# Expert tiles of a mixture-of-experts layer: from transposes on the matrix engine to transposing loads of 16-bit halves

## The chip, the cores and the metric

The kernel runs on one core of a Trainium2 chip. The metric is device microseconds (us) of one execution. A core has engines that run side by side, each through its own list of instructions in order: TensorE (PE in the profile, with its weight loads as PEld), VectorE (DVE), ScalarE (ACT), GpSimd (POOL) and SyncE (SP), which here only issues DMA transfers. Transfers are carried by 16 DMA engines that all issuers share.

## The reference, cut to what matters

The reference takes 16,384 tokens of 256 numbers (32 blocks of 512) through three parts.

```
h = tokenizer(x)                                  # a DFT of patches and a matrix, here one set of matmuls
h = h + retention_and_mlp(layernorm(h))           # q, k, v, a decaying scan, relu MLP 256 -> 1024 -> 256
tokens = layernorm(h)                             # float32, 256 features
combine = weights of the best 2 of 8 experts      # softmax of tokens @ router_w.T, top 2, renormalized
out = tokens
for e in range(8):
    y = gelu(tokens @ w1[e] + b1[e]) @ w2[e] + b2[e]
    out = out + combine[:, e:e+1] * y
h = h + out
```

Every token goes to two experts, so the expert part handles 32,768 rows.

## The kernel before, in words

**Blocks.** The tokens are worked on in 32 blocks of 512 (`TT` = 4 groups of 128 partitions). The main loop has 34 iterations; in each, three blocks are at different stages: a new one is embedded and goes through retention, a middle one through the MLP, an old one is routed. The order of instructions on SP, PE, DVE and ACT is the order of the Python code (a schedule written out by hand); POOL's is left to the planner.

**Where expert rows come from.** At the end of the MLP (`mlp_out`, L345 to L375) the normalized tokens are written to the tile `tok` (L363, L364), which has 260 numbers per token: 256 features and four more, the key of the first expert, two shares and the token's number. `choose` and `place` (L393 to L477) work out which two experts a token goes to and at which row of the scratch buffer `xbuf` in HBM it belongs. Eight indirect DMAs per block, issued by POOL (L450), scatter the 1,040-byte rows into `xbuf`, where each expert has a region of its own.

**Expert tiles.** `take` (L496) cuts the filled parts of the regions into tiles of 256 rows (135 in all) and appends them to a list. `expert_step` (L637) advances the list by one tile. In step n it runs:

- `load` (L556) of the tile three places ahead. SP reads the expert's and the row's offset from a table, issues the load of the rows as `xg` (L561; 260 KB, rows on the partitions, six buffers) and then the load of the expert's weights `w` (L566; 641.5 KB, five buffers).
- `turn` (L568) of tile n+1: four PE transposes of 128x128 (L572) bring the rows into features-first order in PSUM, and one ACT copy (L574) takes them to `xT`.
- `enter` (L576) of tile n: eight matmuls (L581), and the Gelu on ACT (L589).
- `leave` (L593) of tile n-1: eight matmuls (L598); DVE works out each row's share (L607, L610) from the extra numbers in `xg`, adds the bias and scales (L612, L614) into `y` (two buffers); POOL issues two indirect DMAs (L618) that add the rows of `y` to `out` in HBM, at the token numbers in `xg`. The two adds of a tile wait until both adds of the tile before have landed (L616), so that no sum is lost.

An `xg` buffer is free again when the adds of its tile have landed, because these read the token numbers from it. A `w` buffer is free when L612 has read the output bias from it.

**Steps in an iteration.** While there is a new block, `slot` (L651) runs an expert step in each of four places, as long as more than 12 tiles are waiting: after `embed`, after the fourth `mlp_in`, after the retention and after `residual`. Once no blocks are left, the remaining tiles are worked off one after another (L710). A backlog of about 12 tiles and the last block's 18 are therefore done near the end.

**Around `mlp_out`.** At the end of an iteration the order of ACT's list is: the two `ks` activations of the retention, the expert steps' copies and Gelus; then, at the start of the next iteration, the copy `ms` (L262), which frees a PSUM buffer of the pool `p_tm` (three buffers) and lets DVE form the new block's `h` (L276); the two `hT` activations of `features2` (L221), then the two `tokT` copies of `features3` (L215), which free buffers of the pool `p_mm` (four). `turn`, `enter`, `features2`, `features3` and every `feature_mm` take their PSUM tiles from `p_mm` in turn.

Of the kernel before, what the change touches and what calls it, by code (L numbers as in the profile page):

```python
# [11 lines left out]

F32 = mybir.dt.float32
I32 = mybir.dt.int32
AF = mybir.ActivationFunctionType
ALU = mybir.AluOpType
AX = mybir.AxisListType

P = 128
# [10 lines left out]
def vit_tower_kernel(  # L30
# [15 lines left out]
    nc = tc.nc  # L46
    B, NBLK, _, XW = x.shape
    D = wtok.shape[1]
# [3 lines left out]
    KD, KH = D // P, H // P  # L52
    J = STRIDE // 2
    TT = 4
# [8 lines left out]
    S = 2 * P  # L63
# [3 lines left out]
    RW = D + 4  # L67
# [166 lines left out]
    class Block:  # L234
# [110 lines left out]
        def mlp_out(self, u):  # L345
            if u == 0:
                self.norm = Norm()
            ps = p_tm.tile([P, 2, D], F32, name="tm")
            for i in range(2):
                for k in range(KH):  # L350
                    nc.tensor.matmul(  # L351
                        ps[:, i, :],
                        lhsT=self.aT[:, k, ts(u * 2 + i, P)],
                        rhs=w2_sb[:, k, :],
                        start=k == 0,
                        stop=k == KH - 1,
                    )
            nc.vector.tensor_tensor(self.h[:, ts(u, 2), :], ps, self.h[:, ts(u, 2), :], ALU.add)  # L358
            for i in range(2):
                self.norm.stats(self.h, u * 2 + i)  # L360
            if u == U - 1:
                self.norm.factors()
                self.tok = two.tile([P, TT, RW], F32, name="tok")  # L363
                self.norm.apply(self.tok, self.h)  # L364
                nc.vector.tensor_tensor(self.h, self.h, self.tok[:, :, :D], ALU.add)

                to = out[ts(self.i, BLK), :].rearrange("(u q r) d -> q u (r d)", q=P, r=2)
                self.stored = nc.sync.dma_start(out=to, in_=self.h.rearrange("p (u r) d -> p u (r d)", r=2))
                unordered("sums", self.stored, ())
                nc.gpsimd.iota(  # L370
                    self.tok[:, :, NUMBER : NUMBER + 1].bitcast(I32),
                    pattern=[[2 * P, U], [1, 2]],
                    base=self.i * BLK,
                    channel_multiplier=2,
                )  # L375
# [17 lines left out]
        def choose(self):  # L393

            ps = self.lg
            shape = [P, TT, E]

            def wide(a):
                return a.unsqueeze(2).to_broadcast(shape)

            lg = small.tile(shape, F32, name="lg")
            top = small.tile([P, TT], F32, name="top")
            first_key = self.tok[:, :, FIRST]
            nc.vector.tensor_copy(lg, ps)
            nc.vector.tensor_reduce(top, lg, AX.X, ALU.max)
            nc.vector.tensor_tensor(lg, lg, wide(top), ALU.subtract)
            key = small.tile(shape, F32, name="key")
            self.oh = oh = small.tile([P, 2, TT, E], F32, name="oh")
            nc.vector.scalar_tensor_tensor(key, lg, 0.0, key0, ALU.is_equal, ALU.mult)
            nc.vector.tensor_reduce(first_key, key, AX.X, ALU.max)  # L410
            nc.vector.tensor_tensor(oh[:, 0], key, wide(first_key), ALU.is_equal)
            nc.vector.scalar_tensor_tensor(lg, oh[:, 0], -3.0e38, lg, ALU.mult, ALU.add)
            second = small.tile([P, TT], F32, name="second")
            nc.vector.tensor_reduce(second, lg, AX.X, ALU.max)
            nc.vector.tensor_tensor(key, lg, wide(second), ALU.is_equal)
            nc.vector.tensor_tensor(key, key, key0, ALU.mult)
            nc.vector.tensor_reduce(top, key, AX.X, ALU.max)
            nc.vector.tensor_tensor(oh[:, 1], key, wide(top), ALU.is_equal)
            self.both = small.tile(shape, F32, name="both")
            nc.vector.tensor_tensor(self.both, oh[:, 0], oh[:, 1], ALU.add)  # L420
            self.ex = small.tile([P, TT], F32, name="ex")
            nc.gpsimd.tensor_tensor(self.ex, euler, second, ALU.pow)

        def place(self):
# [5 lines left out]
            before = small.tile([P, TT, E], F32, name="before")  # L430
            nc.vector.tensor_copy(before[:, 0, :], cnt)
            for t in range(TT):
                to = cnt if t == TT - 1 else before[:, t + 1, :]
                nc.vector.tensor_tensor(to, ps[:, 1, t, :], before[:, t, :], ALU.add)
            nc.vector.tensor_tensor(before, ps[:, 0], before, ALU.add)
            nc.vector.tensor_tensor(oh, oh, before.unsqueeze(1).to_broadcast([P, 2, TT, E]), ALU.mult)
            row = small.tile([P, 2, TT], I32, name="row")
            rowf = small.tile([P, 2, TT], F32, name="rowf")
            nc.vector.tensor_reduce(rowf, oh, AX.X, ALU.add)
            nc.vector.tensor_copy(row, rowf)  # L440

            share = small.tile([P, TT], F32, name="share")
            nc.vector.tensor_scalar(share, self.ex, 1.0, None, ALU.add)
            nc.vector.reciprocal(share, share)
            nc.vector.tensor_tensor(self.tok[:, :, SECOND], share, self.ex, ALU.mult)
            nc.vector.tensor_tensor(self.tok[:, :, DIFF], share, self.tok[:, :, SECOND], ALU.subtract)
            writes = []
            for t in range(TT):
                for c in range(2):
                    write = nc.gpsimd.indirect_dma_start(  # L450
                        out=xbuf,
                        out_offset=bass.IndirectOffsetOnAxis(ap=row[:, c, t : t + 1], axis=0),
                        in_=self.tok[:, t, :],
                        in_offset=None,
                    )
                    unordered("rows", write, ())
                    writes.append(write)
            if self.i == 0:
                spare = xbuf[E * REG :, :].rearrange("(i p c) d -> p i (c d)", i=SPARE, p=P)
                to = none.rearrange("p c d -> p (c d)").unsqueeze(1).to_broadcast([P, SPARE, 2 * RW])  # L460
                write = nc.sync.dma_start(out=spare, in_=to)
                unordered("rows", write, ())
                writes.append(write)
                write = nc.sync.dma_start(
                    out=out[NTOK:, :].rearrange("(p c) d -> p c d", p=P), in_=none[:, :, :D]
                )
                unordered("sums", write, ())
            if self.i == NB - 1:
                ends = small.tile([1, E], I32, name="ends")
                nc.vector.tensor_copy(ends, cnt[0:1, :])  # L470
                for e in range(E):
                    end = nc.sync.value_load(ends[:, e : e + 1], min_val=e * REG, max_val=e * REG + NTOK)
                    to = xbuf[bass.ds(end, S), :].rearrange("(p c) d -> p c d", p=P)
                    write = nc.sync.dma_start(out=to, in_=none)
                    unordered("rows", write, ())
                    writes.append(write)
            return writes  # L477
# [13 lines left out]
        after(what, others)  # L491
        tc.add_to_no_dep_group(name, what.ins)

    xbuf = dram.tile([ROWS, RW], F32, name="xbuf")

    def take(n, block, writes):  # L496

# [52 lines left out]
    class Tile:  # L550
# [5 lines left out]
        def load(self):  # L556
            t = self.t
            wrow = nc.sync.value_load(self.table[:, 0, t : t + 1], min_val=0, max_val=(E - 1) * P)
            row = nc.sync.value_load(self.table[:, 1, t : t + 1], min_val=0, max_val=ROWS - S)
            self.xg = six.tile([P, 2, RW], F32, name="xg")  # L560
            read = nc.sync.dma_start(  # L561
                out=self.xg, in_=xbuf[bass.ds(row, S), :].rearrange("(c p) d -> p c d", p=P)
            )
            unordered("rows", read, self.writes)
            self.w = five.tile([P, NW], F32, name="w")
            nc.sync.dma_start(out=self.w, in_=wex[bass.ds(wrow, P), :])  # L566

        def turn(self):  # L568
            ps = p_mm.tile([P, KD, 2, P], F32, name="mm")
            for k in range(KD):  # L570
                for c in range(2):
                    nc.tensor.transpose(ps[:, k, c, :], self.xg[:, c, ts(k, P)], ident)  # L572
            self.xT = two.tile([P, KD, S], F32, name="xT")
            nc.scalar.copy(self.xT, ps.rearrange("p k c q -> p k (c q)"))  # L574

        def enter(self):  # L576
            self.ge = two.tile([P, KD, S], F32, name="ge")
# [15 lines left out]
        def leave(self):  # L593
            w = self.w
            ps = p_tm.tile([P, 2, D], F32, name="tm")
            for c in range(2):
# [8 lines left out]
            share = small.tile([P, 2], F32, name="tile_share")  # L605
            tag = w[:, 5 * D + KD : 5 * D + KD + 1]
            nc.vector.scalar_tensor_tensor(  # L607
                share, self.xg[:, :, FIRST], tag, self.xg[:, :, DIFF], ALU.is_equal, ALU.mult
            )
            nc.vector.tensor_tensor(share, share, self.xg[:, :, SECOND], ALU.add)  # L610
            y = two.tile([P, 2, D], F32, name="y")
            nc.vector.tensor_tensor(y, ps, w[:, 4 * D : 5 * D].unsqueeze(1).to_broadcast([P, 2, D]), ALU.add)  # L612
            for c in range(2):
# [3 lines left out]
            for c in range(2):  # L617
                add = nc.gpsimd.indirect_dma_start(  # L618
                    out=out,
                    out_offset=bass.IndirectOffsetOnAxis(  # L620
                        ap=self.xg[:, c, NUMBER : NUMBER + 1].bitcast(I32), axis=0
                    ),
                    in_=y[:, c, :],
                    in_offset=None,
# [169 lines left out]
```

## Time and profile before

| what | value |
|---|---|
| median of three executions | 2452.55 us (2449.38 to 2454.42) |
| profiled execution, its own time | 2448.38 us |
| span of the profiled execution (first to last instruction) | 2446.4 us |
| PE busy | 2298.4 us (94%) |
| DVE busy | 1347.3 us (55%) |
| POOL busy | 930.1 us (38%) |
| ACT busy | 556.7 us (23%) |
| moved by DMA | 256.44 MB, mean 105 GB/s |

Busy time is a share of the whole span, and the stages of this kernel have different limits, so the table alone does not tell what sets the end. The page's strip of 40 slices shows each engine's busy share over the span in tenths. The answers on a stretch of the timeline list instructions with start, duration, engine and line; "idle before" behind an instruction says how long its engine had waited and for whom. A busy time of PE includes the modelled end of the last matmul, which lies over the start of the next group, so what a group takes from PE's time is better read from the distance between starts.

### The profile page before, as it was taken

The numbers are of one execution on the slowest core, as the hardware profiler recorded it, in microseconds if no ns is written. First come the engines' busy times: TensorE is split into PE (matmuls) and PEld (weight loads), VectorE is DVE, ScalarE is ACT, GpSimd is POOL, SyncE is SP. The second block draws the span as 40 slices with busy tenths as digits, with TensorE's granted clock in tenths as the row PEclk, the third lists the DMA queues.
The fourth block names the chain that finished last, engine by engine and source line by source line (L and its number), as shares of the span: only waits on it lengthen the run. The fifth ranks groups of instructions, "written<-read, shape, count | busy, mean of one in ns | idle before, by whom it ended". The sixth has DMA issues, their size and how long they took to land. (4 is left out here: it accounts for less than half of the span.)

```text
span 2446.4 us, 29049 instructions
## 1 busy us (share of the span) xinstructions
PE 2298.4 (94%) x9740; PEld 1687.8 (69%) x9740; DVE 1347.3 (55%) x4111; ACT 556.7 (23%) x952; POOL 930.1 (38%) x845
## 2 busy tenths in 40 slices
PE   3999999999999999999999999999999999986673
PEld 2677666777777777777777777777777777665553
DVE  6566665565655555655555556555555665533221
ACT  0122222222222222222222222222222222221221
POOL 0022222344444334444443344444433444335444
PEclk8999999999999999999999999999999999998887
DMA  4021121333344343333443433334334333347674
GB/s 140 18 79 59 56 105 64 98 89 102 109 122 116 103 110 101 89 102 109 122 113 105 112 101 89 102 109 122 111 107 111 102 90 85 91 106 208 168 182 86
DMA packets 128181, 256.44 MB, mean 105 GB/s; under 512 B 14497, under 2 KB 88097, under 8 KB 123937
## 3 DMA queue, kind: packets, MB, share of 16 engines
q1 hardware_dynamic: 76864, 185.09, 23.3%
q0 software_dynamic: 51168, 69.50, 15.3%
q8 instruction: 77, 1.26, 0.2%
q14 instruction: 72, 0.58, 0.1%
HBM read 164.04 MB, written 90.50 MB: 104 GB/s over the span
## 5 line engine op out<-in xcount | busy, mean ns | idle before, releaser
L618 POOL DMA_INDIRECT out<-y,xg x270 | 426.1, 1578 | 587.6 <-DVE y L614 386.9
L229 PE MATMUL mm<-hT,w_sb 128*128 128x512 f32 x1024 | 478.3, 600 | 0.0
L351 PE MATMUL tm<-w_sb,aT 128*128 128x256 f32 x2048 | 453.0, 379 | 0.0
L351 PEld LDWEIGHTS tm<-w_sb,aT 128*128 128x128 f32 x2048 | 388.5, 190 | 54.9 <-issue 2.4
L450 POOL DMA_INDIRECT xbuf<-tok,row x256 | 314.4, 1228 | 238.1 <-DVE whole L506 161.5
L229 PE MATMUL mm<-hT,wqkv_sb 128*128 128x512 f32 x768 | 338.1, 596 | 0.1
L612 DVE TENSOR_TENSOR y<-tm,w 128x512 f32<-128x512 f32 x135 | 93.3, 691 | 382.8 <-PE tm L598 226.9
L229 PEld LDWEIGHTS mm<-hT,w_sb 128*128 128x128 f32 x1024 | 184.6, 190 | 158.4 <-issue 155.4
L581 PE MATMUL mm<-xT,w 128*128 128x256 f32 x1080 | 275.9, 401 | 3.5 <-DVE ret L313 2.3
L191 POOL TENSOR_SCALAR rstd<-mv 128x4 f32<-128x4 f32 x96 | 37.1, 387 | 635.8 <-DVE mv L185 635.8
L343 ACT ACTIVATE aT<-mm,vec 128x512 f32<-128x512 f32 x256 | 175.9, 687 | 395.2 <-PE mm L229 392.6
L229 PEld LDWEIGHTS mm<-hT,wqkv_sb 128*128 128x128 f32 x768 | 143.9, 191 | 169.6 <-issue 154.1
L598 PE MATMUL tm<-w,ge 128*128 128x256 f32 x1080 | 258.4, 383 | 0.0
L269 PE MATMUL tm<-weff,xd 128*128 128x256 f32 x1024 | 233.4, 382 | 8.5 <-DVE xd L246 8.5
L581 PEld LDWEIGHTS mm<-xT,w 128*128 128x128 f32 x1080 | 206.2, 201 | 34.6 <-DVE ret L313 9.2
L598 PEld LDWEIGHTS tm<-w,ge 128*128 128x128 f32 x1080 | 209.1, 194 | 29.9
L269 PEld LDWEIGHTS tm<-weff,xd 128*128 128x128 f32 x1024 | 191.1, 192 | 32.7 <-DVE xd L246 8.9
L574 ACT COPY xT<-mm 128x512 f32<-128x512 f32 x135 | 79.0, 585 | 531.3 <-PE mm L572 528.2
L589 ACT ACTIVATE ge<-mm,w 128x256 f32<-128x256 f32 x270 | 113.1, 470 | 182.7 <-PE mm L581 157.2
L572 PE MATMUL mm<-ident,xg 128*128 128x128 f32 x540 | 85.1, 282 | 64.9 <-DMA xg<-xbuf 64.8
L258 PE MATMUL tm<-wsum,xb 128*128 128x256 f32 x512 | 118.3, 385 | 25.8 <-ACT wsum L115 25.8
L358 DVE TENSOR_TENSOR h<-tm,h 128x512 f32<-128x512 f32 x64 | 44.0, 687 | 174.8 <-PE tm L351 174.8
(112 smaller groups left out, 2277.2 us busy)
## 6 DMA issues: line engine op xcount, KB each, us to landing
w<-in_wex SPq DMA_DIRECT2D x135, 641.5 KB
xg<-xbuf SPq DMA_DIRECT2D x135, 260.0 KB
xb<-in_x SPq DMA_DIRECT2D x32, 1040.0 KB
out<-h SPq DMA_DIRECT2D x32, 512.0 KB
out<-y,xg POOLq DMA_INDIRECT x270
xbuf<-tok,row POOLq DMA_INDIRECT x256
xbuf<-none SPq DMA_DIRECT2D x8, 260.0 KB
w_sb<-in_w SPq DMA_DIRECT2D x2, 1024.0 KB
```

The source lines that it names most:

```text
L229: nc.tensor.matmul(ps, lhsT=w[:, k, ts(m, P)], rhs=rhs[:, k, :], start=k == 0, stop=k == KD - 1)
L258: nc.tensor.matmul(ps[:, u, :], lhsT=od[:, j, ts(u, P)], rhs=wsum[:, j, :], start=j == 0, stop=j == J - 1)
L269: nc.tensor.matmul(ps[:, i, :], lhsT=xd[:, i, j, ts(u, P)], rhs=weff[:, i * J + j, :], start=j == 0, stop=j == J - 1,)
L343: nc.scalar.activation(self.aT[:, m, :], ps, AF.Relu, bias=vec[:, MB1 + m : MB1 + m + 1])
L351: nc.tensor.matmul(ps[:, i, :], lhsT=self.aT[:, k, ts(u * 2 + i, P)], rhs=w2_sb[:, k, :], start=k == 0, stop=k == KH - 1,)
L450: write = nc.gpsimd.indirect_dma_start(out=xbuf, out_offset=bass.IndirectOffsetOnAxis(ap=row[:, c, t : t + 1], axis=0), in_=self.tok[:, t, :],
L572: nc.tensor.transpose(ps[:, k, c, :], self.xg[:, c, ts(k, P)], ident)
L581: nc.tensor.matmul(ps[:, m, :], lhsT=self.w[:, k * D + m * P : k * D + (m + 1) * P], rhs=self.xT[:, k, :], start=k == 0, stop=k == KD - 1,)
L589: nc.scalar.activation(self.ge[:, m, :], ps[:, m, :], AF.Gelu, bias=self.w[:, 5 * D + m : 5 * D + m + 1])
L598: nc.tensor.matmul(ps[:, c, :], lhsT=self.ge[:, k, ts(c, P)], rhs=w[:, (2 + k) * D : (3 + k) * D], start=k == 0, stop=k == KD - 1,)
L612: nc.vector.tensor_tensor(y, ps, w[:, 4 * D : 5 * D].unsqueeze(1).to_broadcast([P, 2, D]), ALU.add)
L618: add = nc.gpsimd.indirect_dma_start(out=out, out_offset=bass.IndirectOffsetOnAxis(ap=self.xg[:, c, NUMBER : NUMBER + 1].bitcast(I32), axi ...
```

## The change

The rows of `xbuf` are stored in another form, and are read back already turned.

- In `mlp_out` the normalized tokens go to `tok` without the four extra numbers and with one buffer instead of two. ACT then makes a second tile, `row`, of the same 1,040 bytes per token: the first 512 bytes hold the upper 16-bit halves of the 256 features, the next 512 bytes the lower halves, the last 16 bytes the four extra numbers. This takes two ACT copies of 16-bit words per block, of 128x1024 each (new L371), with a stride of two words on the reading side. The row writes take `row` instead of `tok`.
- `load` issues three transfers instead of two: a transposing load of the two planes of 16-bit words (256 rows of 512 words) into `xh`, laid out 128 partitions x 4 x 256 (six buffers); then `w`; then a load of only the four extra numbers of each row into `xg` (16 bytes a row).
- `turn` has no PE instruction any more. Two ACT copies of 128x512 16-bit words put the upper and the lower halves of the features together in `xT` (new L580), with a stride of two words on the writing side.
- The shares and the token numbers are read from the small `xg`. Names change in `place` (`row` to `to`, `to` to `upto`); the arithmetic does not.

```diff
@@ mlp_out
-                self.tok = two.tile([P, TT, RW], F32, name="tok")
+                self.tok = one.tile([P, TT, D], F32, name="tok")
                 self.norm.apply(self.tok, self.h)
-                nc.vector.tensor_tensor(self.h, self.h, self.tok[:, :, :D], ALU.add)
+                nc.vector.tensor_tensor(self.h, self.h, self.tok, ALU.add)
+
+                self.row = two.tile([P, TT, RW], I32, name="row")
+                halves = self.tok.rearrange("p t d -> p (t d)").bitcast(U16).rearrange("p (t d i) -> p t d i", t=TT, i=2)
+                for i in range(2):
+                    nc.scalar.copy(self.row.bitcast(U16)[:, :, i * D : (i + 1) * D], halves[:, :, :, 1 - i])
...
@@ place
                     write = nc.gpsimd.indirect_dma_start(
                         out=xbuf,
-                        out_offset=bass.IndirectOffsetOnAxis(ap=row[:, c, t : t + 1], axis=0),
-                        in_=self.tok[:, t, :],
+                        out_offset=bass.IndirectOffsetOnAxis(ap=to[:, c, t : t + 1], axis=0),
+                        in_=self.row[:, t, :],
                         in_offset=None,
                     )
...
@@ Tile.load and Tile.turn
-            self.xg = six.tile([P, 2, RW], F32, name="xg")
-            read = nc.sync.dma_start(
-                out=self.xg, in_=xbuf[bass.ds(row, S), :].rearrange("(c p) d -> p c d", p=P)
-            )
+            self.xh = six.tile([P, 2 * KD, S], U16, name="xh")
+            rows = xbuf[bass.ds(row, S), :]
+            read = nc.sync.dma_start(out=self.xh, in_=rows.bitcast(U16)[:, : 2 * D], transpose=True)
             unordered("rows", read, self.writes)
             self.w = five.tile([P, NW], F32, name="w")
             nc.sync.dma_start(out=self.w, in_=wex[bass.ds(wrow, P), :])
+            self.xg = six.tile([P, 2, RW - D], I32, name="xg")
+            read = nc.sync.dma_start(out=self.xg, in_=rows[:, D:].rearrange("(c p) d -> p c d", p=P))
+            unordered("rows", read, self.writes)
 
         def turn(self):
-            ps = p_mm.tile([P, KD, 2, P], F32, name="mm")
-            for k in range(KD):
-                for c in range(2):
-                    nc.tensor.transpose(ps[:, k, c, :], self.xg[:, c, ts(k, P)], ident)
             self.xT = two.tile([P, KD, S], F32, name="xT")
-            nc.scalar.copy(self.xT, ps.rearrange("p k c q -> p k (c q)"))
+            halves = self.xT.rearrange("p k s -> p (k s)").bitcast(U16).rearrange("p (k s i) -> p k s i", k=KD, i=2)
+            for i in range(2):
+                nc.scalar.copy(halves[:, :, :, 1 - i], self.xh[:, i * KD : (i + 1) * KD, :])
...
@@ Tile.leave
-                share, self.xg[:, :, FIRST], tag, self.xg[:, :, DIFF], ALU.is_equal, ALU.mult
+                share, self.xg.bitcast(F32)[:, :, FIRST - D], tag, self.xg.bitcast(F32)[:, :, DIFF - D], ALU.is_equal, ALU.mult
...
-                        ap=self.xg[:, c, NUMBER : NUMBER + 1].bitcast(I32), axis=0
+                        ap=self.xg[:, c, NUMBER - D : NUMBER - D + 1], axis=0
```

In the program that is built from it, the transposing load is one instruction of SP per tile, which names a piece of 16 rows by 128 words as its unit.

More of the change, by code (lines that the diff above doesn't have):

```diff
@@ L14 @@
 I32 = mybir.dt.int32
+U16 = mybir.dt.uint16
 AF = mybir.ActivationFunctionType
@@ L370, in mlp_out @@
                 nc.gpsimd.iota(
-                    self.tok[:, :, NUMBER : NUMBER + 1].bitcast(I32),
+                    self.row[:, :, NUMBER : NUMBER + 1],
                     pattern=[[2 * P, U], [1, 2]],
@@ L402, in choose @@
             top = small.tile([P, TT], F32, name="top")
-            first_key = self.tok[:, :, FIRST]
+            first_key = self.row.bitcast(F32)[:, :, FIRST]
             nc.vector.tensor_copy(lg, ps)
@@ L432, in place @@
             for t in range(TT):
-                to = cnt if t == TT - 1 else before[:, t + 1, :]
-                nc.vector.tensor_tensor(to, ps[:, 1, t, :], before[:, t, :], ALU.add)
+                upto = cnt if t == TT - 1 else before[:, t + 1, :]
+                nc.vector.tensor_tensor(upto, ps[:, 1, t, :], before[:, t, :], ALU.add)
             nc.vector.tensor_tensor(before, ps[:, 0], before, ALU.add)
             nc.vector.tensor_tensor(oh, oh, before.unsqueeze(1).to_broadcast([P, 2, TT, E]), ALU.mult)
-            row = small.tile([P, 2, TT], I32, name="row")
+            to = small.tile([P, 2, TT], I32, name="to")
             rowf = small.tile([P, 2, TT], F32, name="rowf")
             nc.vector.tensor_reduce(rowf, oh, AX.X, ALU.add)
-            nc.vector.tensor_copy(row, rowf)
+            nc.vector.tensor_copy(to, rowf)
             share = small.tile([P, TT], F32, name="share")
@@ L444, in place @@
             nc.vector.reciprocal(share, share)
-            nc.vector.tensor_tensor(self.tok[:, :, SECOND], share, self.ex, ALU.mult)
-            nc.vector.tensor_tensor(self.tok[:, :, DIFF], share, self.tok[:, :, SECOND], ALU.subtract)
+            nc.vector.tensor_tensor(self.row.bitcast(F32)[:, :, SECOND], share, self.ex, ALU.mult)
+            nc.vector.tensor_tensor(self.row.bitcast(F32)[:, :, DIFF], share, self.row.bitcast(F32)[:, :, SECOND], ALU.subtract)
             writes = []
@@ L459, in place @@
                 spare = xbuf[E * REG :, :].rearrange("(i p c) d -> p i (c d)", i=SPARE, p=P)
-                to = none.rearrange("p c d -> p (c d)").unsqueeze(1).to_broadcast([P, SPARE, 2 * RW])
-                write = nc.sync.dma_start(out=spare, in_=to)
+                zeros = none.rearrange("p c d -> p (c d)").unsqueeze(1).to_broadcast([P, SPARE, 2 * RW])
+                write = nc.sync.dma_start(out=spare, in_=zeros.bitcast(I32))
                 unordered("rows", write, ())
@@ L472, in place @@
                     end = nc.sync.value_load(ends[:, e : e + 1], min_val=e * REG, max_val=e * REG + NTOK)
-                    to = xbuf[bass.ds(end, S), :].rearrange("(p c) d -> p c d", p=P)
-                    write = nc.sync.dma_start(out=to, in_=none)
+                    pad = xbuf[bass.ds(end, S), :].rearrange("(p c) d -> p c d", p=P)
+                    write = nc.sync.dma_start(out=pad, in_=none.bitcast(I32))
                     unordered("rows", write, ())
@@ L492, in unordered @@
         tc.add_to_no_dep_group(name, what.ins)
-    xbuf = dram.tile([ROWS, RW], F32, name="xbuf")
+    xbuf = dram.tile([ROWS, RW], I32, name="xbuf")
     def take(n, block, writes):
@@ L607, in leave @@
             nc.vector.scalar_tensor_tensor(
-                share, self.xg[:, :, FIRST], tag, self.xg[:, :, DIFF], ALU.is_equal, ALU.mult
+                share, self.xg.bitcast(F32)[:, :, FIRST - D], tag, self.xg.bitcast(F32)[:, :, DIFF - D], ALU.is_equal, ALU.mult
             )
-            nc.vector.tensor_tensor(share, share, self.xg[:, :, SECOND], ALU.add)
+            nc.vector.tensor_tensor(share, share, self.xg.bitcast(F32)[:, :, SECOND - D], ALU.add)
             y = two.tile([P, 2, D], F32, name="y")
```

## The prediction

> **What bounds the kernel now.** I read the page's strip of 40 slices first, to see whether one engine sets the whole span.
>
> ```profile
> PE   3999999999999999999999999999999999986673
> POOL 0022222344444334444443344444433444335444
> DMA  4021121333344343333443433334334333347674
> ```
>
> PE is full from slice 2 to about slice 35, then falls to 6 or 7 tenths while POOL and DMA rise. These are two stages with different limits, so I asked for the busy times of a stretch of each.
>
> ```profile
> core 0: us, PE busy (x) PEld busy (x) DVE busy (x) ACT busy (x) POOL busy (x), PEclk, DMA share, GB/s
> 440.00:2190.00 1750.00, 1741.37 (x7492) 1285.75 (x7491) 1011.39 (x3132) 421.32 (x722) 712.48 (x626) 1.00 0.39 104
> 2250.00:2400.00 150.00, 105.40 (x443) 85.03 (x442) 35.19 (x110) 31.52 (x67) 68.07 (x45) 0.90 0.72 175
> ```
>
> In the first, the **blocks' stage**, PE works 1741 of 1750 us: each microsecond taken from PE's list there is a microsecond of the end, until something else is late. In the second, the **tail**, PE idles almost a third. What does set the end there is told by the chain of waits that ended last, asked for between 2388 and 2416 us:
>
> ```profile
> 2398.06 3.90 DMA out<-y,xg
> ...
> 2402.09 0.70 DVE y L612
> ...
> 2402.80 1.54 POOL out L618
> 2404.34 0.30 issue
> 2404.65 4.25 DMA out<-y,xg
> ```
>
> The adds of one tile land, DVE's L612 runs 0.70, POOL issues the next tile's first add (1.54), 0.30 passes, the second add is issued and lands 4.25 later, and so on. PE is nowhere in it. From 2322.36 to 2409.74 the chain takes 13 turns, 6.72 us each. After the last load, 2409.74 to 2428.98, a turn takes 6.41: all loads together slow the chain by only 0.3 us per tile.
>
> **What is removed from PE.** The timeline of PE around one expert step:
>
> ```profile
> 1098.03 3.62 PE L269 MATMUL tm<-weff,xd 128*128 128x256 f32 x16
> 1101.49 0.60 PE L572 MATMUL mm<-ident,xg 128*128 128x128 f32 x4
> 1101.93 1.89 PE L581 MATMUL mm<-xT,w 128*128 128x256 f32 x8
> ```
>
> The busy time of the four transposes is 0.60, but their starts take 0.44 (1101.49 to 1101.93): the rest is the modelled end of the last one, under L581. The next step gives 0.47 (1113.95 to 1114.42), and in a block's four steps three read 0.44. I take 0.448. By the copies that follow a turn (L574), 101 turns lie between 380 and 2150 us, 3 before 2194 and 31 after it. So 104 x 0.448 = **46.6 us** leave the stage in which PE is the bound. The busy times, 63 us over the same stretch, are the upper end. The other 31 turns are worth nothing: they lie in the tail, beside the chain of adds, and PE waits there 64.8 us for `xg` already, at L572.
>
> What could be late next in the blocks' stage? Busy shares of the next engines, DVE 58%, POOL 41%, ACT 24%, leave room. `xT` is made one step ahead of its use, and the rows are loaded three steps ahead, with steps some 12 to 23 us apart, so a load may land several microseconds later than now before PE sees it.
>
> **What is added to ACT.** A turn has two copies instead of one. L574 takes 585 ns for 128x512; for 16-bit words with a stride I have no row and take the same, from half to double (0.3 to 1.2 us): 135 x 0.585 = 79 us more of ACT, all of it idle time now, since ACT waits 528 us for L572 alone. The row copies (new L371) are 64, of 1024 elements; nearest is L115, 1,058 ns for 128x1024: 68 us. ACT goes from 557 to about 704 us of 2446.
>
> The wait that the row copies bring matters more than their time, because ACT works in order and they stand ahead of `ms`, `hT` and `tokT`. In the iteration at 1020 us DVE ends `tok` at 1026.63. Now `ms` runs at 1023.13; then it would run only after two copies, at 1028.75, `hT` until 1030.8 and `tokT` until 1031.9. Who needs them? DVE's L276 at 1027.81 slips to 1029.4, but its second half is held by PE until 1031.79 anyway. PE comes to L581 at about 1031.6 and needs there the PSUM buffer that the first `hT` frees at 1030.1, at 1033.3 the one that `ms` frees, at 1035 `hT` itself. The margins are 1.5 us and more, so I cost it at nothing; if the cover went, the two copies would be paid, 32 x 2.1 = 68 us. `tok` with one buffer costs nothing: its readers end an iteration before the next write. `row` has two, and POOL's row writes read it a whole iteration later than ACT writes it.
>
> **What the loads become.** This is the unknown, since the trace holds no transposing transfer. Per tile the tail has 6.72 us. In 2250 to 2400 us the hardware queue holds the 16 DMA engines for 41.7% and the software queue for 30.1%; over 22 tiles, 2.84 us per engine and tile for `xg` and `w`, 2.05 for adds, together 4.9. The rows' part is read in a stretch with only such rows (2349.5 to 2350.5):
>
> ```profile
> q1 hardware_dynamic: 168, 0.17, 88.8%
> ```
>
> 0.888 x 16 us over 168 packets is 85 ns for a packet of 1,040 bytes; 16 such per engine make 1.35 us per tile. The new instruction's piece, 16 rows by 128 words, cuts each row into four runs of 256 bytes, 64 per engine. If each costs a whole packet, that is 64 x 85 = 5.4 us, the dear end. At the start of the span there are rows for short packets: 23 to 24 us and 24 to 25 us.
>
> ```profile
> DMA packets 366, 0.34 MB, mean 344 GB/s; under 512 B 31, under 2 KB 366, under 8 KB 366
> q1 hardware_dynamic: 366, 0.34, 109.3%
> ```
>
> ```profile
> DMA packets 556, 0.34 MB, mean 337 GB/s; under 512 B 277, under 2 KB 550, under 8 KB 550
> q1 hardware_dynamic: 556, 0.34, 123.9%
> ```
>
> The first gives 48 ns for packets of about 940 bytes; with that for the 279 longer ones of the second, its 277 short ones take 23 ns each. So the cheap end is 64 x 23 = 1.5 us. I take 29 ns for 256 bytes, on the line between 23 and 48: **1.9 us**; these are packets read from HBM in a burst, as here. The small load of 16 bytes a row is 16 packets per engine, 16 x 23 = 0.4 us (up to 1.35). Together 2.3 for 1.35, or +0.9 us of DMA per tile: 4.9 becomes 5.8 of 6.72 us, still no bound. How much of it the adds feel: all of today's 2.84 costs them 0.3, a tenth; but the loads start when the adds land and end as the next adds begin, so what is longer falls on them. Between 0.1 and 1 I take half, 0.45 us for 31 tiles: **+14 us**. In the blocks' stage DMA is busy 39%, and it is free.
>
> The order of SP's list helps a little: the rows no longer wait for the adds of the tile six before, only the small load does, but the next tile's rows stand behind it in SP's queue, so the burst still starts as adds land. SP's two issues of a tile take about 1 us now (2335.08 to 2336.05), of 6.72.
>
> The row above says a transposing load can be anything from 1.5 to 5.4 us. The Trainium skill, "DMA: Bandwidth & Descriptors", section "Latency and other measured facts", gives 261 GB/s for transposing transfers, which would be an estimate of 1.0 us for 262,144 bytes and an end near 2406 us. "VectorE: DVE Perf Modes", section "The three transpose paths", speaks against the change: 1309 ns for a 128x128 block of 16-bit numbers by DMA against 390 ns on TensorE; eight such blocks in a row, 10.5 us, would put the end near 2700 us. No trace here shows either.
>
> **The sum.** Against the profiled execution: 2448.4 - 46.6 + 14 = 2415.8 us. The median of the runs is 2452.55, 4.2 above that execution, so I forecast 2420 us. This case's own range: 2448.4 - 63 + 3 + 4.2 = 2393 to 2448.4 - 46.6 + 28 + 4.2 = 2434.
>
> **Rivals.**
> - **The tail becomes bound by the transposing load.** One mechanism: each of the 64 runs per engine costs a full packet, 85 ns, the small load's too, so +5.4 us of DMA per tile. If only the engines' capacity counts, a tile takes 10.3 us instead of 6.72, 31 x 3.6 = +112; if all falls into the chain of adds, 31 x 5.4 = +168. That is 2518 to 2574, middle 2546 us: slower. It decides from 46.6 / 31 = 1.5 us more per tile, so from a load of about 2.5 to 3.4 us. For it: the pieces are a quarter as long and no cheap row is a scatter over 128 partitions. Against: the short packets at the start.
> - **SP's issue is long.** L128, 256 runs of 32 bytes, held SP's queue for 4.97 us at the start, though with a full queue ahead. If the transposing load holds SP so long, `w` goes out some 4 us later, onto the adds, 31 x 1.5 = +46 us for the 14 of the forecast: 2448.4 - 46.6 + 46 + 4.2 = 2452 us, no change. In the blocks' stage 4 x 5 us in a block's some 68 would not show.
> - **ACT's order takes PE's gain**: 68 us as worked out, 2488 us. The margins speak against it.
>
> **How the numbers follow.** Forecast 0.55, tail bound 0.30, SP's issue 0.10, ACT's order 0.05. Differences under 0.2% (5 us) can't be told from no change here. The second rival lies on no change, 0.04 faster, 0.03 same, 0.03 slower; so faster 0.59, same 0.03, slower 0.38. The range reaches from the low end of the forecast to 2555, beyond which about 0.12 of the tail-bound case lies.
>
> **What would show it.** Right: no PE instruction at `turn`; the blocks' stage, up to the last row write, 45 us shorter with PE still full; the tail's turn between 6.8 and 7.2 us; the hardware queue's share in the tail a little up. Wrong: turns of 8 us or more with PE or the adds waiting for `xh`; idle time of PE at L229 or L581 for ACT in the blocks' stage; SP held for microseconds at the transposing load. A transposing load that lands tens of microseconds late would make even the blocks' stage wait, and then the time lies above my range.

## The result and the profile after

The changed kernel takes 2468.31 us (median of 4, 2462.99 to 2470.1) against 2452.89 us before; the ratio is 1.0061, 95% interval 1.0041 to 1.0081. The forecast was 2420 us, faster. The profiled execution took 2462.99 us, with a span of 2460.9.

The page's strip for the changed kernel, 40 slices of 61.5 us each:

```profile
PE   3999999999999999999999999999999999865653
POOL 0022322444444444434444444443444444343333
DMA  4021132544545554554444455545554434485664
```

PE stops being full one slice earlier than before, and what follows is longer and emptier. The busy times of two stretches of the changed kernel, of which the second is the one that was shown of before:

```profile
core 0: us, PE busy (x) PEld busy (x) DVE busy (x) ACT busy (x) POOL busy (x), PEclk, DMA share, GB/s
440.00:2140.00 1700.00, 1691.04 (x7082) 1242.65 (x7080) 1014.66 (x3132) 531.31 (x864) 733.15 (x626) 1.00 0.49 107
2250.00:2400.00 150.00, 90.42 (x255) 69.39 (x254) 25.50 (x80) 33.17 (x64) 48.38 (x32) 0.75 0.62 127
```

In the blocks' stage PE is as full as it was. In the tail every engine is less busy than before, DMA too: 0.62 for 0.72. So no engine has become the bound; something makes them wait. (PEclk, the clock granted to TensorE, is lower too, 0.75 for 0.90, but PE is not in the chain that sets the end.) A clean mark between the two stages is the end of POOL's last row write: 2237.3 us before, 2192.5 now. The blocks' stage is **44.8 us shorter**. The rest, from that mark to the end of the span, went from 209.1 to 268.4 us: the tail is **59.3 us longer**. The chain that ended last, in the changed kernel:

```profile
2305.85 1.54 POOL out L624
2307.39 0.30 issue
2307.70 6.47 DMA out<-y,xg
...
2314.29 0.70 DVE y L618
...
2315.01 1.54 POOL out L624
2316.55 0.30 issue
2316.85 6.32 DMA out<-y,xg
```

It is the same chain with the same links but one: from the issue of the second add to its landing it takes 5.8 to 7.7 us while there are loads, where it took 3.8 to 4.4. Of the 29 turns after the mark, the middle 18 take 9.48 us on average (6.81 before). Once the loads are over, the last four turns take 6.43, as before (6.51). So the loads hold up the adds. When they go out is seen in SP's queue, here in the changed kernel:

```profile
2314.28 0.38 SPq L573 DMA_DIRECT2D xg<-xbuf  x1
2315.98 1.27 SPq L568 DMA_TRANSPOSE xh<-xbuf  x1
2317.51 0.35 SPq L571 DMA_DIRECT2D w<-in_wex  x1
```

and in the kernel before:

```profile
2348.46 0.38 SPq L561 DMA_DIRECT2D xg<-xbuf  x1
2349.10 0.33 SPq L566 DMA_DIRECT2D w<-in_wex  x1
```

In both, the first line is the moment when the adds of a tile land and free an `xg` buffer. That SP stands there waiting is in its waits over the whole span (us in total, times, longest), before and changed:

```profile
SPq L561 <- DMA out<-y,xg: 385.6, 75, 7.3
SPq L573 <- DMA out<-y,xg: 196.9, 48, 6.5
```

Before, the rows went out at once and the weights 0.6 us later. Now only the small load goes out at once. Behind it in SP's list stand the next tile's two value loads (they fill the 1.3 us up to the next line), the transposing load (issued 1.70 us after the landing, 1.27 us long) and the weights (3.23 us after the landing).

What that does is seen in what each queue moved in single microseconds. In the kernel before, from the second to the third and from the fourth to the fifth microsecond after the landing at 2348.46 (the hardware queue q1 carries loads, the software queue q0 the adds; after the name stand packets, MB and the share of 16 engines' time, which can pass 100% in so short a stretch):

```profile
q1 hardware_dynamic: 175, 0.40, 112.2%
```

```profile
q0 software_dynamic: 148, 0.14, 116.7%
q1 hardware_dynamic: 7, 0.01, 1.6%
```

First the loads, then the adds: they take turns. In the changed kernel, from the fourth to the fifth, from the sixth to the seventh and from the seventh to the eighth microsecond after the landing at 2314.28:

```profile
q1 hardware_dynamic: 958, 0.27, 135.5%
q0 software_dynamic: 30, 0.02, 10.3%
```

```profile
q1 hardware_dynamic: 71, 0.36, 88.5%
q0 software_dynamic: 15, 0.02, 10.0%
```

```profile
q0 software_dynamic: 122, 0.11, 72.2%
q1 hardware_dynamic: 34, 0.10, 27.5%
```

The first add's packets are through by the first of these stretches (16 and 98 in the two microseconds ahead of it, 30 in it); in the stretch between the first two no packet of an add moves, and the second add's move only as rows and weights have passed.

### The profile page after: what moved, and what is told of

It reads as the page before. It is cut to its first block, busy times and chain, and to the rows that moved or that the text cites. A ratio compares the mean times of both kernels' runs of the same rounds, so it can differ in the third digit from the quotient of the medians.

```text
span 2460.9 us, 28451 instructions
## 1 busy us (share of the span) xinstructions
PE 2265.2 (92%) x9200; PEld 1654.1 (67%) x9200; DVE 1351.6 (55%) x4111; ACT 706.8 (29%) x1151; POOL 954.2 (39%) x845
## 5 line engine op out<-in xcount | busy, mean ns | idle before, releaser
L456 POOL DMA_INDIRECT xbuf<-row,to x256 | 338.5, 1322 | 179.9 <-DVE full L514 102.6
L587 PE MATMUL mm<-xT,w 128*128 128x256 f32 x1080 | 298.7, 426 | 107.0 <-DMA w<-in_wex 99.9
L587 PEld LDWEIGHTS mm<-xT,w 128*128 128x128 f32 x1080 | 223.5, 213 | 159.9 <-issue 105.0
L604 PE MATMUL tm<-w,ge 128*128 128x256 f32 x1080 | 269.4, 395 | 2.0 <-DVE y L618 2.0
L604 PEld LDWEIGHTS tm<-w,ge 128*128 128x128 f32 x1080 | 218.3, 202 | 37.0 <-issue 2.4
L270 PE MATMUL tm<-weff,xd 128*128 128x256 f32 x1024 | 233.5, 382 | 8.4 <-DVE xd L247 8.4
L580 ACT COPY xT<-xh 128x512 uint16<-128x512 uint16 x270 | 187.5, 767 | 184.2 <-DMA xh<-xbuf 184.2
L371 ACT COPY row<-tok 128x1024 uint16<-128x1024 uint16 x64 | 63.8, 1044 | 546.7 <-issue 356.4
L270 PEld LDWEIGHTS tm<-weff,xd 128*128 128x128 f32 x1024 | 191.2, 192 | 32.6 <-DVE xd L247 8.8
```

What stands on the lines that cost most here:

```text
L270: nc.tensor.matmul(ps[:, i, :], lhsT=xd[:, i, j, ts(u, P)], rhs=weff[:, i * J + j, :], start=j == 0, stop=j == J - 1,)
L456: write = nc.gpsimd.indirect_dma_start(out=xbuf, out_offset=bass.IndirectOffsetOnAxis(ap=to[:, c, t : t + 1], axis=0), in_=self.row[:, t, ...
L580: nc.scalar.copy(halves[:, :, :, 1 - i], self.xh[:, i * KD : (i + 1) * KD, :])
L587: nc.tensor.matmul(ps[:, m, :], lhsT=self.w[:, k * D + m * P : k * D + (m + 1) * P], rhs=self.xT[:, k, :], start=k == 0, stop=k == KD - 1,)
L604: nc.tensor.matmul(ps[:, c, :], lhsT=self.ge[:, k, ts(c, P)], rhs=w[:, (2 + k) * D : (3 + k) * D], start=k == 0, stop=k == KD - 1,)
```

## The experiments

Two theories stood at the start. **A**: the place of the loads in SP's list makes the loss. **B**: the transposing transfer itself does. "Blocks" is the end of the last row write, "tail" the rest of the span, "turn" the mean of the middle 18 turns, "rows" and "weights" the issue after a landing, in us, all of the profiled execution. Each ratio is to runs of the kernel before made together with that run (medians 2449.94 to 2453.1 us).

| run | median us | ratio to before (95%) | blocks | tail | turn | rows | weights |
|---|---|---|---|---|---|---|---|
| before | 2452.89 | | 2237.3 | 209.1 | 6.81 | 0.0 | 0.6 |
| changed | 2468.31 | 1.0061 (1.0041 to 1.0081) | 2192.5 | 268.4 | 9.48 | 1.7 | 3.2 |
| small_load_first | 2450.19 | 0.9996 (0.9986 to 1.0006) | 2192.5 | 256.8 | 8.78 | 0.5 | 2.1 |
| plain_rows | 2433.81 | 0.9918 (0.9901 to 0.9934) | 2192.6 | 241.6 | 8.28 | 2.0 | 2.4 |
| split_before | 2480.6 | 1.0119 (1.0103 to 1.0136) | 2241.1 | 237.2 | 7.98 | 2.0 | 2.4 |
| twelve_small | 2439.99 | 0.9947 (0.993 to 0.9964) | 2192.4 | 245.1 | 8.44 | 3.1 | 0.8 |
| small_weights_rows | 2431.25 | 0.9914 (0.9898 to 0.9931) | 2190.6 | 239.0 | 8.02 | 1.1 | 0.7 |
| seven_weights | 2434.13 | 0.9928 (0.9912 to 0.9945) | 2191.2 | 239.8 | 8.28 | 3.2 | 0.8 |
| tail_on_pe | 2401.97 | 0.9803 (0.9786 to 0.9819) | 2185.3 | 210.5 | 6.93 | 0.0 | 0.6 |
| plain_small_weights | 2405.1 | 0.9823 (0.9807 to 0.9839) | 2186.0 | 216.4 | 7.09 | 1.2 | 0.6 |
| late_weights_before | 2501.44 | 1.0216 (1.0199 to 1.0233) | 2242.3 | 256.1 | 8.82 | 0.0 | 2.9 |

The end of the blocks' stage spreads over 7 us among the kernels with the change and 5 among those without; that is left unexplained.

**small_load_first.** The four extra numbers are loaded ahead of the rows.

```diff
+            tags = nc.sync.dma_start(out=self.xg, in_=rows[:, D:]...)
             read = nc.sync.dma_start(out=self.xh, ..., transpose=True)
             nc.sync.dma_start(out=self.w, ...)
-            read = nc.sync.dma_start(out=self.xg, in_=rows[:, D:]...)
```

> The changed kernel with the order of a tile's three loads altered: the four extra numbers first, then the transposing load, then the weights. Theory A (place in SP's list): in the tail the small load waits for the adds of the tile six before, and the next tile's value loads, transposing load and weights stand behind it, so they go out 1.7 and 3.25 us after the adds land and their transfers fall on the next adds. With the small load in front, the value loads are done while SP waits anyway, the transposing load goes out 0.4 and the weights some 2 us after the landing, and a turn of the tail falls from 9.4 us to between 7 and 8: 2410 to 2440 us in all. Theory B (the transposing transfer itself is too dear for the DMA engines): the turn stays at 9 or more, 2455 to 2470 us.

2450 us and a turn of 8.78: neither theory's number. The place of the loads matters, but this order leaves the weights behind the long issue of the transposing load, at 2.1 us, and gains only 0.7 us a turn.

**plain_rows.** The transposing load becomes a plain one, in the same place. The kernel leaves out the turning; the bytes are the same, and the two copies of `turn` read the planes where they now lie.

```diff
-            read = nc.sync.dma_start(out=self.xh, in_=rows.bitcast(U16)[:, : 2 * D], transpose=True)
+            read = nc.sync.dma_start(out=<xh as p c d>, in_=rows.bitcast(U16)[:, : 2 * D].rearrange("(c p) d -> p c d", p=P))
```

> The changed kernel with a plain load of the same bytes in place of the transposing one, in the same place of SP's list; xT then holds rows that are not turned, so the experts' results are wrong. Theory A: the turn of the tail stays well above the 6.7 us of the kernel before, 8 us or more, 2435 to 2465 us, since the order of the loads is unchanged; only the shorter issue (0.4 for 1.3 us) and 1.2 us of DMA per tile are saved. Theory B: the turn falls to 6.7 to 7 us and the whole to 2400 to 2412 us.

Without any transposing transfer the turn is still 8.28 us, and the tail 32.5 us longer than before. The other 26.8 of the 59.3 us go with the transposing load: its transfer, and its longer issue, which also puts the weights at 3.2 instead of 2.4 us. Theory B alone is refuted, and A alone explains about half.

**split_before.** The kernel before with the order of the change.

```diff
-            read = nc.sync.dma_start(out=self.xg, in_=<260 numbers a row>)
+            read = nc.sync.dma_start(out=self.xf, in_=rows[:, :, :D])
             nc.sync.dma_start(out=self.w, ...)
+            read = nc.sync.dma_start(out=self.xg, in_=rows[:, :, D:])
```

> The kernel before, with its load of a tile's rows split as in the change: the 256 features first (plain, six buffers), then the weights, then the four extra numbers (six buffers of their own); the transposes stay on PE. Theory A: the tail's turn grows as in the changed kernel, by 1.5 to 2.5 us over some 28 tiles, so 2490 to 2520 us. Theory B: nothing of the transposing transfer is in it, so 2450 to 2460 us.

The split alone lengthens the tail by 28 us and the whole by 1.2%, less than A expected, with the transposes still on PE. The order does harm without the rest of the change.

**twelve_small** and **seven_weights.** More buffers: twelve for the extra numbers, then also seven for the weights.

```diff
-            self.xg = six.tile([P, 2, RW - D], I32, name="xg")
+            self.xg = twelve.tile([P, 2, RW - D], I32, name="xg")
```

```diff
-    five = ctx.enter_context(tc.tile_pool(name="five", bufs=5))
+    five = ctx.enter_context(tc.tile_pool(name="five", bufs=7))
```

> The changed kernel with twelve buffers instead of six for the four extra numbers, so that the small load waits for adds six tiles further back. Theory A: SP is no longer held at the small load, but five weight buffers still hold it until L618 of the tile five before has run, 0.7 us after an adds' landing; the transposing load of the next tile then goes out later than the weights. The turn changes to between 7.5 and 9 us, 2420 to 2460 us. Theory B: the turn stays at 9 us or more, 2455 to 2470 us.

> The changed kernel with twelve buffers for the four extra numbers and seven instead of five for the weights. Theory A2: SP always runs ahead until some buffer is missing, and in the tail each buffer comes free at a landing of adds, so deeper buffers leave the loads where they are, 0.8 to 3 us after a landing: a turn of 8.2 to 8.7 us as with twelve small buffers alone, 2432 to 2446 us. Theory B2 (with enough buffers the loads come loose from the landings and fill the gaps of the DMA engines): turns under 7.3 us, 2400 to 2418 us.

Both came out as the place theory expected. With twelve small buffers SP is held at the weights instead, whose buffer the addition of the bias (old L612) frees just after a landing, so the weights go first and the rows last. Seven weight buffers leave the weights at 0.8 and the rows at 3.2 us: the loads are still let go by a landing, only a landing of an earlier tile. Its turn of 8.28 is not a gain over 8.44: the last loads go out earlier here, and the last two of the 18 turns (6.81 and 6.32) come with the last tile's weights and with no load; the other 16 take 8.49.

**small_weights_rows.** The weights no longer stand behind the transposing load.

```diff
             read = nc.sync.dma_start(out=self.xg, in_=rows[:, D:]...)
             nc.sync.dma_start(out=self.w, ...)
             read = nc.sync.dma_start(out=self.xh, ..., transpose=True)
```

> The changed kernel with the loads of a tile in the order four extra numbers, weights, transposing load. With the small load in front the tail's turn was still 8.8 us. Theory A1 (the transposing load's 1.27 us of issue in SP's queue pushes the weights onto the adds): now the weights go out 0.5 us after the adds land, the turn falls to about 7.5 us and the whole to 2410 to 2430 us. Theory B1 (the transfer of the transposing load itself, beside the adds on the same DMA engines, holds the adds up, wherever its issue stands): it still falls on the adds, the turn stays between 8.4 and 9.2 us, 2440 to 2458 us.

2431.25 us and a turn of 8.02, between the two. Taking the weights from behind the transposing load is worth 0.76 us a turn against small_load_first; more than 1 us over the turn of before is left.

**plain_small_weights.** The same order with a plain load of the rows, which closes a square. The turning is again left out.

> The order four extra numbers, weights, rows again, now with a plain load of the same bytes for the rows (xT holds rows that are not turned, so the experts' results are wrong). Completes a square of two orders and two kinds of load: in the changed kernel's order the turn of the tail is 9.5 us with the transposing and 8.3 with the plain load; in this order 8.0 with the transposing one. If place and kind add up, this turn is 6.8 to 7.1 us, the whole 2400 to 2412 us. If the transposing load costs something only where it falls on the adds, and does not here, the turn stays near 8 and the whole over 2420 us.

It adds up. The turns of the square:

| order | plain load | transposing load |
|---|---|---|
| rows, weights, small | 8.28 | 9.48 |
| small, weights, rows | 7.09 | 8.02 |

The order is worth 1.2 to 1.5 us a turn, the kind of load 0.9 to 1.2, nearly independent of each other. In the second row the loads are issued at nearly the same moments (weights at 0.6 and 0.7 us, rows at 1.2 and 1.1), so its 0.9 is not a matter of place. What three transfers in place of two cost by themselves is at most the 0.28 us between 7.09 and the 6.81 of before.

**late_weights_before.** The kernel before, with nothing but the weights' issue moved.

```diff
+            for _ in range(4):
+                nc.sync.value_load(self.table[:, 0, t : t + 1], ...)
             self.w = five.tile([P, NW], F32, name="w")
             nc.sync.dma_start(out=self.w, ...)
```

> The kernel before with four more value loads of SP between a tile's rows and its weights, whose results nobody uses: no transfer is added, only the weights go out some 3.2 us after the adds land instead of 0.6. Theory A (place alone is enough): the turn of the tail grows by 0.7 to 1.5 us, 2470 to 2495 us. Theory C (SP's place of the load does not matter, only the added transfers do): 2449 to 2457 us.

This is the sharpest of them: no transfer is added, and the turn grows by 2.0 us, more than expected, the whole by 2.2%. SP's queue and the chain of this kernel:

```profile
2345.80 0.38 SPq L561 DMA_DIRECT2D xg<-xbuf  x1
2348.69 0.33 SPq L568 DMA_DIRECT2D w<-in_wex  x1
```

```profile
2346.51 1.54 POOL out L620
2348.05 0.31 issue
2348.36 5.89 DMA out<-y,xg
```

The rows go out with the landing and the weights 2.89 us after it, as the second add has just been issued (2348.36); the add then lands after 5.89 us.

**tail_on_pe.** The change for the first 104 tiles, the old way for the last 31: rows and extra numbers in one plain load ahead of the weights, two ACT copies that put the halves together, PE transposes, one ACT copy.

```diff
+            self.late = at["load"] >= FULL[NB] - 31
+            if self.late:
+                read = nc.sync.dma_start(out=self.xr, in_=rows)
+                self.xg = self.xr[:, :, D:]
...
+                for k in range(KD):
+                    for c in range(2):
+                        nc.tensor.transpose(ps[:, k, c, :], xf[:, c, ts(k, P)], ident)
```

> The changed kernel, but the last 31 of the 135 tiles are loaded plainly as in the kernel before (rows with the extra numbers in one load, then the weights), put together by two ACT copies and turned by PE. If the gain lies in the blocks' stage and the whole loss in the tail's loads, the blocks' stage ends 45 us earlier than in the kernel before and the tail lasts about 209 us as there: 2400 to 2415 us. If the loss had another source in the change (ACT's order, the row copies, the halves), the tail stays over 235 us: 2435 us or more.

2401.97 us, 2.0% faster than before and the fastest of the kernels that turn the rows. A turn of its chain:

```profile
2324.27 0.70 DVE y L641
...
2325.28 1.54 POOL out L647
2326.82 0.31 issue
2327.13 3.89 DMA out<-y,xr
```

The last link is back to 3.89 us. The tail lasts 210.5 us, as before the change, although the row copies and the halves are all still there: nothing else in the change lengthens it.

## Why the prediction was wrong, step by step

- **Two stages with different limits: right.** PE bounds the blocks' stage, the chain of adds the tail.
- **The gain: right.** 46.6 us were forecast; the mark moved by 44.8. The starts on PE show it: L270 (old L269) at 1008.72 and L587 (old L581) at 1012.17, 3.45 us apart, where 3.90 had lain between them. Busy time would have said 63. (The stretch shown ends before the eighth matmul of L587.)

```profile
1008.72 3.62 PE L270 MATMUL tm<-weff,xd 128*128 128x256 f32 x16
1012.17 1.67 PE L587 MATMUL mm<-xT,w 128*128 128x256 f32 x7
```

- **ACT: right.** The copies of L580 take 767 ns (0.3 to 1.2 us were allowed), those of L371 1,044 (1,058 were taken from L115), ACT is busy 706.8 us (704 forecast). That this sum came so near is in part luck: the copies of L580 are busy 187.5 us where 158 was taken, and ACT's groups add up to some 735 us, which overlap in time. `ms` does come late: DVE waits 39.7 us for it at L277, 1.3 us a block. PE's waits between 440 and 2140 us are 7 us in all, 1.4 of them for ACT. The cover held.
- **The cost of the transposing load on the DMA engines: nearly right.** The hardware queue's share went from 23.3% of 2446.4 to 30.0% of 2460.9 us, 168 us or 1.25 us a tile (0.9 forecast). Against plain_rows, which differs in the kind of load alone (24.8% of 2434.2), it is 1.0 us a tile. The queue's packets, MB and share, in the changed kernel and in plain_rows:

```profile
q1 hardware_dynamic: 219424, 185.11, 30.0%
q1 hardware_dynamic: 113584, 185.10, 24.8%
```

In the other such pair, small_weights_rows and plain_small_weights (30.7% of 2429.6 us, 24.7% of 2402.4), it is 1.1. The order of the loads moves it as well: small_load_first, at 28.3% of 2449.3 us, stands only 0.7 us a tile above plain_rows. In the prediction's own stretch of the tail, 2250 to 2400 us, the hardware queue holds the engines 38.7% for 16 tiles, 3.63 us a tile, where it was 2.84: 0.8 more. Against plain_rows the packets grew by 784 a tile, from 256 to 1,024 and 16 more, so the four runs per row that the prediction cut from the piece are what is moved. With the 1.35 us of the plain rows a transposing load holds each engine an estimated 2.35 us, 37 ns a run, where 29 was taken and 23 to 85 allowed.

- **The step that failed** is "the next tile's rows stand behind it in SP's queue, so the burst still starts as adds land", and with it "Between 0.1 and 1 I take half, 0.45 us for 31 tiles: +14 us". The term measured +59.3 us, in two parts. 32.5 us stay with a plain load in the same place (plain_rows): most of that is the place of the loads (the other order takes the tail from 241.6 to 216.4, plain_small_weights), which the prediction put at nothing and even took for a small help. The other 26.8 come with the transposing load: about 1 us more of each DMA engine a tile makes a turn 0.9 to 1.2 us longer in the square, so the adds feel nearly all of it and not half (0.9 us felt whole by 31 tiles is 28, the top of the forecast's own range).

  What moved the loads: the burst starts 1.7 us after the landing, and its larger part, the weights, 3.2 us after it. SP's work of the next tile, hidden before in the wait for the adds, came to lie behind that wait. late_weights_before shows that weights which go out 2.9 instead of 0.6 us after the landing cost 2 us a turn by themselves, without any added transfer. The prediction had read the cause in the trace, that loads start when adds land and end as the next adds begin, and had priced only a longer burst, not a later one: the 0.3 us a tile that it read for all loads is their price when they go out with the landing, and not their price later.

- **The rivals.** That the tail's DMA engines become full did not happen: they are busy 0.62. The load's 2.35 us stay below the 2.5 from which this rival was to decide, and with the 26.8 us of the transposing load alone the sum would be 2448.4 - 44.8 + 26.8 = 2430.4, still a gain. (That rival's upper end, 3.4, does not follow from its terms: by capacity alone it is 1.35 + 6.72 - 4.9 + 1.5 - 0.4 = 4.3 us.) The rival of SP's issue had the right mechanism, weights that go out later and fall on the adds. It was taken for the long issue alone: that is 1.27 us and not 5, and the value loads and the wait ahead of them do the rest (in late_weights_before four value loads move the weights by 2.3 us). Its 46 us, in place of the forecast's 14, would have given no change; with the 59.3 that were measured the sum is 2448.4 - 44.8 + 59.3 = 2462.9, the profiled execution's time, as it must be for two stages that make up the span. That 2468 us still lies below 2555, the top of the stated range, is luck: that end was set for a tail with full DMA engines, which did not come.

The Trainium skill, "DMA: Bandwidth & Descriptors", section "Latency and other measured facts", gives 261 GB/s for transposing transfers with a non-contiguous middle dimension, measured on one kernel; that is an estimate of 1.0 us for such a load. Here it held the engines an estimated 2.35 us, 112 GB/s. "VectorE: DVE Perf Modes", section "The three transpose paths", gives 1309 ns for a 128x128 block by DMA, an estimate of 10.5 us for eight in a row; here one load of eight blocks held the engines those 2.35 us.

## What to carry to other kernels

When a chain of transfers sets the pace, the moment at which the other transfers go out counts as much as their bytes: find what lets them go, and list every instruction of the issuing queue that comes to stand behind that wait, register loads and long issues too. Splitting a load so that its small part waits and the next large part stands behind it moves the large part in time, even where the bytes stay the same. A resource that is scarce in one stage can be idle in the next, so a change that trades one engine for another is best made only in the stage where it pays, as tail_on_pe does.

## What the runs showed of the hardware

- The adds do not share the DMA engines evenly with a burst of weights. In late_weights_before, in the three microseconds from the fourth to the seventh after the landing at 2345.80, the queues moved:

```profile
q1 hardware_dynamic: 40, 0.21, 89.7%
q0 software_dynamic: 1, 0.00, 0.1%
```

```profile
q1 hardware_dynamic: 64, 0.32, 94.9%
q0 software_dynamic: 2, 0.00, 3.2%
```

```profile
q0 software_dynamic: 96, 0.09, 59.2%
q1 hardware_dynamic: 34, 0.11, 29.6%
```

Not all of the first two is waiting. POOL's instruction for the second add ends at 2349.91, and with no loads about (2411 to 2414 us of the kernel before) an add's first packets come some 0.5 us after that end, which would be about 2350.4 here. They come at 2351.7, so the add was held a little over 1 us. Why it waits for the burst to pass is not settled by these runs.

- A transposing load takes 1.26 to 1.28 us (median) of SP's queue to issue, against 0.37 to 0.38 for a plain one of the same bytes in plain_rows and plain_small_weights (0.14 in the tail of plain_rows).
- ACT's copies of 128x512 16-bit words from SBUF with a stride on the writing side take 767 ns, longer than the 585 ns of 128x512 float32 words from PSUM.
